# Layer 3 attention of a four-layer gated network: order of scores, last sums, projections and tokens within a step

## The chip, the cores and the metric

The kernel runs on one core of one Trainium2 chip. The metric is device time in microseconds (us) for one execution of the whole program; lower is better. Engines are named as in the profile: PE is TensorE's matmul, PEld its weight load, DVE is VectorE, ACT is ScalarE, POOL is GpSimd, SP is SyncE, which issues most of the DMAs.

## The reference

The input is 128 sequences of 64 tokens of width 128, with a context of the same size. Four layers follow one another, each a gated cross attention on the context and then a gated feed-forward part. The attention of layer 3 has 16 heads of width 8 and, in place of softmax, a "stablemax":

```python
def stablemax(x):
    s = jnp.where(x >= 0, x + 1.0, 1.0 / (1.0 - x))
    return s / jnp.sum(s, axis=-1, keepdims=True)
q = query @ Wq.T + bq          # query: the layer norm of x
k = key_value @ Wk.T + bk      # key_value: the context
v = key_value @ Wv.T + bv
scores = jnp.einsum('bhqd,bhkd->bhqk', q, k) / np.sqrt(HD).astype(np.float32)
attn = stablemax(scores)
context = jnp.einsum('bhqk,bhkd->bhqd', attn, v)
return context @ Wo.T + bo
```

The result, times tanh of a gate, is added to x. The feed-forward part of layer 3 sends each token to one of eight experts, up to a capacity; its routing (a layer norm, logits, the best expert, a place in that expert's list) is computed per tile while the attention runs, and its expert stage starts when all tokens are scattered to their slots. The input x of layer 3's attention is itself the sum of x and two rows per token that layer 2's experts wrote.

## The kernel before, in words

x stays on the chip as 64 tiles of 128 tokens (two sequences each). Layer 3's attention (`head_steps`, the branch `layer == 3`) runs a loop over n. A step n, also called a half, covers two tiles, that is four sequences with all heads; there are 32 such steps. Two steps share a group g of four tiles, for which the projections are made: `head_tokens` (normalized tokens xn by POOL, L719; adding the output bias to x by POOL, L726; and the DMA that loads the context ctxT of the group after, L177), `head_transpose` (pxn on PE, L734, xnT on ACT, L736), `head_queries` (pq on PE, L761, two copies qm on ACT, L764), `head_keys` (pk on PE, L773, two operations kx on DVE, L776) and `head_new_values` (pv on PE, L785, four copies vb on ACT, L792). `piece(n, late)` puts one of these into each half of a step. Before the change an even step holds tokens and the transpose in its first half and the new values in its second; an odd step holds the queries and then the keys. They are for the group after the one whose scores are in work.

The work of a step itself is: 16 score matmuls into four PSUM tiles sb (L875); four operations low on DVE, the negative part of the scores (L882); for each of the four quarters j a Ln and an Exp on ACT (L889, L891), which make 1 / (1 - x), and a sum on DVE (L894), which adds the positive part and leaves the weights aT. For the step before (n - 1) the same step computes the values pav (L908) from aT, raw on ACT (L913), the transposes po (L924), the reciprocal r and o on DVE (L930, L941), the transposes pot (L948), oT on ACT (L950), the output py (L968), and on DVE the addition to x (L970) and the statistics st (L200) of two tiles.

Two more streams are laid into the steps by lists of due times: `outputs`, the sums of x with layer 2's expert rows on POOL (L1884), their statistics gst on DVE (L1899, L1903), a group variance gn on DVE, its root on ACT and the norms gn_r (L260); and `first`, the routing of groups of 16, 8 or 4 tiles: variance and norms on DVE, tokens fxn on POOL (L1086), transposes prt (L1525) and logits plg (L1534) on PE, rT on ACT (L1527), the choice and the places on DVE with pup on PE (L1135). `scatter` puts the DMAs that carry routed tokens to their slots on POOL (L1646).

PE, ACT and DVE execute layer 3's attention in the order in which the program writes it (`manual_schedule`); the order on POOL and SP is chosen by the scheduler at build time. PSUM holds five buffers for score tiles and a ring of three ("av") for all the others in the stage.

Of the kernel before, what the change touches and what calls it, by code (L numbers as in the profile page):

```python
# [41 lines left out]
class Net:  # L42
# [536 lines left out]
    def head_steps(self, layer, w, NH):  # L579


        proj, mT, aT, raw, o = {}, {}, {}, {}, {}
        self.ctxT = {}
        self.context(0)

        def piece(n, late):

            g, step = (n // 2 + 1, n % 2) if layer == 3 else ((n + 3) // 2, (n + 1) % 2)
            if 4 * g >= self.NT:
                return  # L590
            if g not in proj:
                proj[g] = {}
                self.head_tokens(g, layer, w, proj[g])
            step = 2 * step + late
            if layer == 3:
                step = (0, 3, 1, 2)[step]
            if step == 0:
                self.head_transpose(g, proj[g])
            elif step == 1:
                self.head_queries(g, w, proj[g])  # L600
            elif step == 2:
                self.head_keys(g, w, proj[g])
                if layer == 2:
                    self.head_mask(g, proj[g])
            else:
                self.head_new_values(g, w, proj[g])

        proj[0] = {}
        outputs = {}
        if layer != 2:  # L610
            outputs = self.outputs_plan(layer)
            for step in sorted(outputs):
                if step[0] < (-2 if layer == 3 else 0):
                    for do in outputs.pop(step):
                        do()
        self.head_tokens(0, layer, w, proj[0])
        self.head_transpose(0, proj[0])
        self.head_keys(0, w, proj[0])
        if layer == 2:
            self.head_mask(0, proj[0])  # L620
        self.head_queries(0, w, proj[0])
        self.head_new_values(0, w, proj[0])
        if layer == 3:


            first = self.first_plan(3)
            for n in range(-2, NH + 8):
                for do in outputs.pop((n, 0), ()):
                    do()
                new, old = 0 <= n < NH, 0 <= n - 1 < NH  # L630
                if new:
                    st = self.head_stable(n, proj[n // 2])
                    self.head_stable_exp(st, 0)
                if old:
                    raw = self.head_values(n - 1, aT.pop(n - 1))
                if new:
                    self.head_stable_exp(st, 1)
                    self.head_stable_sum(st, 0)
                    piece(n, False)
                if old:  # L640
                    o = self.head_back(layer, raw)
                for do in first.pop(2 * n, ()):
                    do()
                self.scatter(2 if n < NH else 16)
                if new:
                    self.head_stable_sum(st, 1)
                    self.head_stable_exp(st, 2)
                if old:
                    oT = self.head_turn(o)
                if new:  # L650
                    self.head_stable_sum(st, 2)
                    self.head_stable_exp(st, 3)
                    piece(n, True)
                if old:
                    self.head_output(n - 1, layer, w, oT)
                    if n % 2 == 0:
                        self.first_fill(2 * n - 4)
                for do in first.pop(2 * n + 1, ()):
                    do()
                self.scatter(2)  # L660
                if new:
                    self.head_stable_sum(st, 3)
                    aT[n] = st["aT"]
                for do in outputs.pop((n, 1), ()):
                    do()
            return
        piece(-1, False)
        piece(-1, True)
        mT[0] = self.head_maxima_T(0, self.head_maxima(0, proj[0]))
        choice = self.choice_plan() if layer == 2 else {}  # L670
        scatter = self.scatter if layer == 2 else lambda n: None
        for n in range(NH + 8):
            for do in outputs.pop((n, 0), ()):
                do()
            if n + 1 < NH:
                mx = self.head_maxima(n + 1, proj[(n + 1) // 2])
            if 0 <= n - 1 < NH:
                raw[n - 1] = self.head_values(n - 1, aT.pop(n - 1))
            if n < NH:
                piece(n, False)  # L680
            if 0 <= n - 2 < NH:
                self.head_output(n - 2, layer, w, o.pop(n - 2))
            for do in choice.pop(2 * n, ()):
                do()
            scatter(3 if n < NH else 16)
            if n < NH:
                aT[n] = self.head_softmax(n, proj[n // 2], mT.pop(n))
            if 0 <= n - 1 < NH:
                o[n - 1] = self.head_back(layer, raw.pop(n - 1))
            if n < NH:  # L690
                piece(n, True)
            for do in choice.pop(2 * n + 1, ()):
                do()
            scatter(2)
            if n + 1 < NH:
                mT[n + 1] = self.head_maxima_T(n + 1, mx)
            if 0 <= n - 1 < NH and layer != 2:
                o[n - 1] = self.head_turn(o[n - 1])
            for do in outputs.pop((n, 1), ()):
                do()  # L700
# [162 lines left out]
            self.tc.add_manual_dep(exp.ins, self.table, ORDER, reason="the table is loaded")  # L863
        return aT

    def head_stable(self, n, pr):


        nc, work = self.nc, self.work
        b0 = 4 * (n % 2)  # L870
        sc = [self.ps_sc.tile([P, 4, 2, S], F32, tag="sc", name="sb") for j in range(4)]
        for b in range(4):
            for j in range(4):
                rows = slice(32 * j, 32 * j + 32)
                nc.tensor.matmul(  # L875
                    sc[j][:, b], lhsT=pr["kx"][rows, b0 + b], rhs=pr["qm"][rows, b0 + b],
                    start=True, stop=True,
                )
        lows = []
        for j in range(4):  # L880
            low = work.tile([P, 4, 2, S], F32, tag="low", name="low", bufs=4)
            nc.vector.tensor_scalar(low, sc[j], 0.0, -1e19, ALU.min, ALU.max)  # L882
            lows.append(low)
        aT = work.tile([P, 4, 4, 2, S], F32, tag="aT", name="aT")
        return {"sc": sc, "low": lows, "aT": aT}
# [756 lines left out]
    def scatter(self, n):  # L1642

        nc, tc = self.nc, self.tc
        for rec, row in self.ready[:n]:
            put = nc.gpsimd.indirect_dma_start(  # L1646
                out=self.scatter_dst, out_offset=bass.IndirectOffsetOnAxis(ap=row, axis=0),
                in_=rec, in_offset=None,
            )

            tc.declare_no_dep(put.ins, group=self.scatter_group, reason="rows apart")
            tc.add_to_no_dep_group(self.scatter_group, put.ins)
            for clear in self.scatter_after:
                tc.add_manual_dep(put.ins, clear, WAIT, reason="slots are clear")
            if self.pool_last:
                tc.add_manual_dep(put.ins, self.pool_last, ORDER, reason="GpSimd in this order")
            self.puts.append(put.ins.name)
            self.bundle.append(put.ins.name)
        del self.ready[:n]
# [315 lines left out]
```

## Time and profile before

| | us |
|---|---|
| median of 10 runs | 2862.94 (2859.89 to 2864.77) |
| the profiled execution, its own time | 2868.76 |
| its span on the core | 2866.7 |
| PE busy in the span | 2286.6 (80%) |
| DVE busy | 1571.0 (55%) |
| ACT busy | 1348.5 (47%) |
| POOL busy | 1056.8 (37%) |
| first and last low of layer 3 (start) | 2309.7 and 2675.0 |

The mean granted TensorE clock of the execution is 0.885 of full speed. Durations below come from this one execution; its time lies 5.8 us above the median of the runs.

A line of the groups or of the timeline names the engine, the line of the program, the operation, and what is written and read, as out<-in. In the timeline the first number is the start in the span and the second the duration; a bracket gives the idle time of the engine before it and what ended it. The view of the waits names who waited, for whom, the total, the number of times and the longest.

### The profile page before, as it was taken

Reading aid. Unit: us, or ns where it says so; the run is one execution under the profiler, and the core shown is the slowest. Engines: PE = TensorE matmul, PEld = TensorE weight load, DVE = VectorE, ACT = ScalarE, POOL = GpSimd, SP = SyncE. Lnnn points to the kernel's source line nnn. Section 1 sums busy time; section 2 is a strip of 40 time slices with the busy share of each in tenths; the row PEclk is TensorE's granted clock in tenths of the full one; section 3 lists DMA queues with packets and bytes.
Section 4 is the critical chain, followed back from the end, with each engine's and each line's share of the span. In section 5 each row is a group of like instructions: output and inputs, shape, how many; then the busy total and the mean of one; then the engine's idle time right before and its main releaser. Section 6 shows DMA issues by size and latency. Waiting matters only on the chain.

```text
span 2866.7 us, 68765 instructions
## 1 busy us (share of the span) xinstructions
PE 2286.6 (80%) x28510; PEld 1637.4 (57%) x28510; DVE 1571.0 (55%) x4232; ACT 1348.5 (47%) x2626; POOL 1056.8 (37%) x1297
## 2 busy tenths in 40 slices
PE   4999999999959778983556888884798666777597
PEld 3666666666647557772334666663566445555465
DVE  4445555554542276658874455455455377867532
ACT  2444444444424245555773444442344357665342
POOL 1222233332344521105653134425455652344344
PEclk9999999999979889995778998896899878877599
DMA  9983000000011310000000011111222530101111
GB/s 256 262 226 69 12 21 23 13 24 13 20 51 60 116 39 17 21 10 8 1 1 19 23 36 49 42 33 56 66 75 68 141 94 27 50 27 39 46 53 45
DMA packets 216582, 161.30 MB, mean 56 GB/s; under 512 B 27333, under 2 KB 192080, under 8 KB 216273
## 3 DMA queue, kind: packets, MB, share of 16 engines
q1 hardware_dynamic: 194288, 121.55, 16.4%
q0 software_dynamic: 16640, 32.22, 3.4%
q8 instruction: 226, 3.70, 0.5%
q10 hardware_dynamic: 5344, 3.15, 0.4%
q14 instruction: 84, 0.68, 0.1%
HBM read 68.62 MB, written 86.31 MB: 54 GB/s over the span
## 4 chain that ended last, share of the span: by engine, by line
PE 51%; DVE 15%; POOL 10%; issue 8%; ACT 8%; DMA 6%; SPq 1%; POOLq 0%; DVEq 0%; ACTq 0%
PE pqk L398 8%; PE pv L421 8%; PE py L480 4%; POOL slots L1646 3%; PE sc L440 2%; PE pt L468 2%; PE sb L850 2%; PE ph L1199 2%; PE pav L908 2%; DMA xe<-slots 2%; DMA outs<-ye,to 2%; PE pye L1218 2%; PE sb L857 2%; PE po L924 1%; POOL h L1384 1%
## 5 line engine op out<-in xcount | busy, mean ns | idle before, releaser
L457 POOL TENSOR_TENSOR a<-a,sm 128x1024 f32<-128x1024 f32 x64 | 121.7, 1902 | 490.5 <-DVE sm L456 449.4
L421 PE MATMUL pv<-Wvo,ctxT 128*64 128x512 f32 x1024 | 247.8, 605 | 0.0
L862 ACT ACTIVATE aT<-sb 128x512 f32<-128x512 f32 x256 | 132.1, 602 | 190.6 <-PE sb L857 190.6
L823 DVE TENSOR_REDUCE mpad<-sa 128x8 f32<-128x512 f32 x256 | 158.9, 683 | 111.5 <-PE sa L818 111.5
L447 DVE TENSOR_REDUCE mx<-sc 128x8 f32<-128x512 f32 x128 | 82.4, 685 | 229.3 <-PE sc L440 229.3
L1812 POOL DMA_INDIRECT outs<-ye,to x136 | 133.7, 983 | 132.0 <-DVE ye L1808 101.3
L428 ACT COPY v<-pv 128x512 f32<-128x512 f32 x128 | 75.2, 587 | 179.8 <-PE pv L421 179.7
L1646 POOL DMA_INDIRECT slots<-x_sb,fc_r x128 | 125.1, 977 | 82.3 <-DVE fc_r L1146 31.2
L908 PE MATMUL pav<-aT,vb 128*32 128x64 f32 x6144 | 130.0, 240 | 31.2 <-DVE aT L894 19.1
L719 POOL TENSOR_SCALAR xn<-x_sb,gn_nm,gn_r 128x128 f32<-128x128 f32 x128 | 58.4, 470 | 247.7 <-PE pxn L734 173.4
L1646 POOL DMA_INDIRECT slots<-x_sb,pl_i x64 | 61.6, 963 | 216.8 <-DVE pl_i L1631 163.5
L480 PEld LDWEIGHTS py<-v,aT 128*64 128x64 f32 x2048 | 117.5, 138 | 36.6 <-issue 19.4
L908 PEld LDWEIGHTS pav<-aT,vb 128*32 128x32 f32 x6144 | 109.3, 122 | 50.4 <-DVE aT L894 22.0
L398 PE MATMUL pqk<-xnT,L_Wq 128*128 128x256 f32 x512 | 121.1, 390 | 15.3 <-ACT xnT L390 14.9
L398 PE MATMUL pqk<-ctxT,L_Wk 128*128 128x256 f32 x512 | 121.4, 391 | 13.7 <-issue 13.7
L1769 PE MATMUL ph<-L_gu,xT 128*128 x272 | 130.5, 604 | 0.1
L402 ACT ACTIVATE kT<-pqk 128x512 f32<-128x512 f32 x128 | 76.4, 597 | 110.7 <-PE pqk L398 110.7
L1218 PEld LDWEIGHTS pye<-L_w,hT 128*128 128x128 f32 x1024 | 119.1, 192 | 14.4 <-issue 11.5
L480 PE MATMUL py<-v,aT 128*64 128x128 f32 x2048 | 124.2, 275 | 0.2 <-ACT aT L471 0.2
L1218 PE MATMUL pye<-L_w,hT 128*128 128x128 f32 x1024 | 119.2, 275 | 0.0
L930 DVE RECIPROCAL r<-po 128x32 f32<-128x32 f32 x96 | 34.3, 357 | 154.5 <-PE po L924 154.5
L1199 PE MATMUL ph<-xeT,L_w 128*128 128x512 f32 x256 | 118.3, 606 | 0.0
(325 smaller groups left out, 5828.1 us busy)
## 6 DMA issues: line engine op xcount, KB each, us to landing
slots<-zero SPq DMA_DIRECT2D x80, 528.0 KB, 9.1
ctxT<-in_ctxT_dram SPq DMA_DIRECT2D x64, 256.0 KB, 2.6
y<-outs SPq DMA_DIRECT2D x24, 512.0 KB, 5.4
xe<-slots SPq DMA_DIRECT2D x136, 66.0 KB, 1.9
xe<-slots SPq DMA_DIRECT2D x32, 264.0 KB, 2.8
L_w<-in_L_ffn_W_dram SPq DMA_DIRECT2D x32, 256.0 KB, 6.0
outs<-fxn SPq DMA_DIRECT2D x16, 256.0 KB
out_dram<-x_sb SPq DMA_DIRECT2D x16, 256.0 KB, 2.7
```

Source lines behind the costliest of these rows:

```text
L398: nc.tensor.matmul(ps[:, cc, :], lhsT=wt[:, (c + cc) * P : (c + cc + 1) * P], rhs=rhs, start=True, stop=True,)
L421: nc.tensor.matmul(ps[h * S : (h + 1) * S], lhsT=tok, rhs=w["Wvo"][:, h, cs, :], start=True, stop=True,)
L457: op = nc.gpsimd.tensor_tensor(ah, ah, sm.unsqueeze(2).to_broadcast([P, 16, S]), ALU.mult)
L480: nc.tensor.matmul(py[rows, :], lhsT=aT[:, c, rows], rhs=v[:, b, c, :], start=(c == 0), stop=(c == 7))
L823: nc.vector.reduce_max(mpad[:, j, 0:8], sc[j].rearrange("p b c k -> p (b c) k"), axis=AX.X)
L862: exp = nc.scalar.activation(aT[:, j], sc[j], AF.Exp)
L908: nc.tensor.matmul(pav[32 * j : 32 * j + 32, b, t, :], lhsT=vb[:, 4 * (b0 + b) + j, t, :], rhs=aT[:, j, b, t, :], start=True, stop=True,)
L1199: nc.tensor.matmul(ph, lhsT=w["w1"][:, e, c * P : (c + 1) * P], rhs=x, start=True, stop=True)
L1218: nc.tensor.matmul(py[:, t, :], lhsT=h[:, c, t * P : (t + 1) * P], rhs=w["w2"][:, e, c, :], start=(c == 0), stop=(c == 3),)
L1646: put = nc.gpsimd.indirect_dma_start(out=self.scatter_dst, out_offset=bass.IndirectOffsetOnAxis(ap=row, axis=0), in_=rec, in_offset=None,)
L1769: nc.tensor.matmul(ph.rearrange("p t f -> p (t f)"), lhsT=xT[j // 4][:, j % 4, :], rhs=gu[:, bass.ds(ex[j], 1), :, :].rearrange("p o t f - ...
L1812: put = nc.gpsimd.indirect_dma_start(out=self.outs2, out_offset=bass.IndirectOffsetOnAxis(ap=to[q][:, j % 4 : j % 4 + 1], axis=0), in_=y[: ...
```

## The change

Within a step the following is placed differently.

- The scores of step n + 1 are written at the end of step n, in front of the late piece; `head_stable` takes them ready.
- The pieces are no longer permuted. An even step holds the transpose and then the queries; an odd step the keys and then the new values.
- The late piece stands at the end of the step, behind the output of n - 1, the second half of the routing and the scores.
- Sum 1 stands in front of the first half of the routing, sum 3 in front of the output's addition to x and the second half of the routing.
- The tokens of a group are made at the end of the odd step before, behind the outputs list.

```diff
             step = 2 * step + late
-            if layer == 3:
-                step = (0, 3, 1, 2)[step]
             if step == 0:
                 self.head_transpose(g, proj[g])
...
             first = self.first_plan(3)
+            scores = None
             for n in range(-2, NH + 8):
                 for do in outputs.pop((n, 0), ()):
                     do()
                 new, old = 0 <= n < NH, 0 <= n - 1 < NH
                 if new:
-                    st = self.head_stable(n, proj[n // 2])
+                    st = self.head_stable(scores)
                     self.head_stable_exp(st, 0)
                 if old:
                     raw = self.head_values(n - 1, aT.pop(n - 1))
...
                 if old:
                     o = self.head_back(layer, raw)
+                if new:
+                    self.head_stable_sum(st, 1)
                 for do in first.pop(2 * n, ()):
                     do()
                 self.scatter(2 if n < NH else 16)
                 if new:
-                    self.head_stable_sum(st, 1)
                     self.head_stable_exp(st, 2)
                 if old:
                     oT = self.head_turn(o)
                 if new:
                     self.head_stable_sum(st, 2)
                     self.head_stable_exp(st, 3)
-                    piece(n, True)
+                    self.head_stable_sum(st, 3)
+                    aT[n] = st["aT"]
                 if old:
                     self.head_output(n - 1, layer, w, oT)
...
                 for do in first.pop(2 * n + 1, ()):
                     do()
                 self.scatter(2)
+                if 0 <= n + 1 < NH:
+                    scores = self.head_scores(n + 1, proj[(n + 1) // 2])
                 if new:
-                    self.head_stable_sum(st, 3)
-                    aT[n] = st["aT"]
+                    piece(n, True)
                 for do in outputs.pop((n, 1), ()):
                     do()
+                g = (n + 1) // 2 + 1
+                if n % 2 and n < NH and 4 * g < self.NT:
+                    proj[g] = {}
+                    self.head_tokens(g, layer, w, proj[g])
             return
```

`head_scores` is the first half of the old `head_stable`, the 16 matmuls; `head_stable` keeps the four operations low.

More of the change, by code (lines that the diff above doesn't have):

```diff
@@ L864, in head_softmax, with head_scores @@
         return aT
-    def head_stable(self, n, pr):
-        nc, work = self.nc, self.work
+    def head_scores(self, n, pr):
         b0 = 4 * (n % 2)
@@ L874, in head_stable @@
                 rows = slice(32 * j, 32 * j + 32)
-                nc.tensor.matmul(
+                self.nc.tensor.matmul(
                     sc[j][:, b], lhsT=pr["kx"][rows, b0 + b], rhs=pr["qm"][rows, b0 + b],
@@ L878, in head_stable @@
                 )
+        return sc
+    def head_stable(self, sc):
+        nc, work = self.nc, self.work
         lows = []
```

## The prediction

> **What bounds the kernel now.** I read the page first: the chain that ended last runs through all engines, so no engine is full and the stage must be read by its waits.
>
> ```profile
> PE 51%; DVE 15%; POOL 10%; issue 8%; ACT 8%; DMA 6%; SPq 1%; POOLq 0%; DVEq 0%; ACTq 0%
> ```
>
> The steps of layer 3 lie between 2308 and 2684 us of the span. Of those 376 us a step has 376 / 32 = 11.75. The view of who waited for whom, for that stretch:
>
> ```profile
> ACT low L889 <- DVE low L882: 74.3, 32, 6.1
> ...
> DVE aT L894 <- ACT low L891: 29.4, 24, 2.1
> ...
> PE pxn L734 <- POOL xn L719: 13.3, 6, 3.8
> ...
> PE sb L875 <- DVE kx L776: 12.6, 12, 2.3
> ```
>
> The columns are the total, the times, the longest. ScalarE stands still once per step (74.3 / 32 = 2.3 us) until VectorE has made the first low of the next step; VectorE in turn waits for Exp in most steps. So a step is one loop: low, Ln/Exp of four quarters on ACT, the last sum and the tail on DVE, low again. The timeline of steps 6 (even, from 2374.33) and 7 (odd, from 2382.19), which hold no routing, shows its parts:
>
> ```profile
> 2374.33 2.48 DVE L882 TENSOR_SCALAR low<-sb 128x512 f32<-128x512 f32 x4 [0.25 <-PE sb L875]
> 2375.06 0.63 ACT L889 ACTIVATE low<-low 128x512 f32<-128x512 f32 x1 [3.60 <-DVE low L882]
> ...
> 2378.78 1.06 PE L785 MATMUL pv<-L_xattn_Wv,ctxT 128*128 128x128 f32 x8
> ...
> 2379.59 0.35 ACT L950 COPY oT<-pot 128x256 f32<-128x256 f32 x1
> ...
> 2380.00 0.71 PE L968 MATMUL py<-wog,oT 128*128 128x128 f32 x4 [0.16 <-ACT oT L950]
> 2380.51 0.63 ACT L891 ACTIVATE low<-low 128x512 f32<-128x512 f32 x1
> 2380.64 1.17 PE L875 MATMUL sb<-qm,kx 32*128 32x128 f32 x32
> ...
> 2381.04 1.49 ACT L792 COPY vb<-pv 64x256 f32<-64x256 f32 x4
> ...
> 2381.60 0.67 DVE L894 SCALAR_TENSOR_TENSOR aT<-sb,low 128x512 f32<-128x512 f32 x1
> ...
> 2382.19 2.47 DVE L882 TENSOR_SCALAR low<-sb 128x512 f32<-128x512 f32 x4
> ...
> 2385.91 1.43 ACT L764 ACTIVATE qm<-pq,bqm,m2s 128x512 f32<-128x512 f32 x2
> ...
> 2389.16 1.52 DVE L776 TENSOR_SCALAR kx<-pk,L_xattn_bk,mc 128x512 f32<-128x512 f32 x2
> ```
>
> The even step takes 7.86 us, the odd one 10.62: in the odd one qm stands in the middle of ACT's run, kx in DVE's tail. The vb copies of the even step are free: pv was ready early, and they end while ACT waits for low anyway.
>
> **What moves on PE.** By the order of the instructions the scores of n+1 stay where they were: behind py (and plg, prt) of step n. What moves is the late piece (pv or pq), from in front of py to behind the scores. "A step ahead" thus advances the scores only where kx or a slow pv held them.
>
> **Odd steps, gain.** All times from the step's first low. qm's two copies leave ACT's run (1.33 to the next Ln), but kx now stands on DVE ahead of the reciprocal: sum 0 starts at 2.41, +0.66 kx, +1.43 reciprocal, +0.39 o, +0.43 and 0.45 through pot, so oT starts at 5.86 where it started at 6.24. Exp 3 then ends at 5.86 + 0.25 + 0.67 + 0.63 = 7.41; sum 3, add and two stats take 1.54: the tail (gst, norms) begins at 8.95 where it began at 9.84. Gain 0.89.
>
> **Even steps, loss.** Before, add and stats filled the time until Exp 3; now sum 3 is in front and DVE stands still for it. Exp 3 ends at 6.81; with 1.57 behind it low comes at 8.38 instead of 7.86. Loss 0.52. A pair gains 0.37 by these two.
>
> **The late copies, a new wait.** qm (even) and vb (odd) now wait on ACT for a matmul behind the scores, and the next step's Ln is queued behind them; so is all of Exp, and by it the sums. Even: oT ends at 5.61, py and scores at 7.48, pq 1.12, qm 1.36: the next Ln may start at 9.96, while low allows it at 8.38 + 0.73 = 9.11. Wait 0.85. Odd: oT ends at 6.22, scores at 8.09, pv and vb 2.55: 10.64 against 9.68. Wait 0.96. A DVE tail of that length hides it; without the tail all of it is paid: an even step passes it on whole, an odd one by 0.6 (low to low 8.95 with Ln at 0.73, 9.45 with Ln at 1.58). Those are full-clock durations. At half clock py takes 1.06 and the scores 2.09 (+1.27), and pq about 2.0 (+0.9): the wait is then 2.1 to 3.1.
>
> **The clock.** Windows of one 3.41 us period each:
>
> ```profile
> 2365.45:2368.86 3.41, 1.51 (x8) 0.89 (x8) 2.68 (x6) 3.35 (x7) 0.00 (x0) 1.00 0.00 0
> 2368.86:2372.28 3.42, 1.98 (x9) 0.98 (x8) 2.24 (x4) 2.54 (x5) 0.00 (x0) 0.50 0.26 77
> 2372.28:2375.69 3.41, 3.41 (x88) 3.19 (x92) 3.06 (x10) 0.63 (x1) 1.43 (x4) 0.50 0.02 5
> 2375.69:2379.10 3.41, 2.13 (x33) 1.59 (x26) 3.10 (x6) 3.32 (x7) 3.33 (x7) 1.00 0.00 0
> ```
>
> Behind the length stand the busy times (and counts) of PE, PEld, DVE, ACT and POOL, then the granted clock, the DMA share and GB/s. A period with PE busy for 1.51 us of 3.41 (44%) was followed by half clock, a full one by full clock. After the change py, scores, pq or pv, pav and pxn or pk stand in one block (0.7 + 1.2 + 1.1 + 1.1 + 0.7), and some 3.6 us with only po and pot (0.66 + 0.41, 30%) follow. A period that falls into these is thinner than the 44%, so I take the block's first matmuls, py and scores, at half clock in some 65% of the steps; now the score rows of the timeline show 2.0 to 2.1 in 12 of 32 steps, 1.4 to 1.8 in 5 more.
>
> [...]
>
> **Sum, steps 1 to 9.** Tails behind the stats are 0, 0.86, 1.83, 0.57 in turn. Four steps 4 to 7 at full clock: +0.6, -1.1, +0.9, -0.4 = 0. With every score run at half clock +4. I take +2.5 per four steps: +5.
>
> **Sum, steps 10 to 28 (routing).** Steps 10, 18, 22 and 26 are held by pxn waiting for POOL (up to 3.8 us), after which pv at half clock (1.9 us) holds py. Now pv is out of the way, and by POOL's order xn stands four fxn (1.74) earlier in steps 10 and 22 and two x_sb adds (1.28 each) earlier in 18: -2.7, -3.9, -1.1, -1.6, together -9. Of the nine odd steps six gain 0.8 to 1.4 each, since a tail hides the copies; 11, 19 and 27, which carry plg and prt in front of the scores, lose 0.3 each: together -6. The six other even steps have tails of 1.3 to 5 us; there sum 3 in front costs 0.5, and the inherited wait 0.7 to 1.7: +9. Half clock where the copies bind, nine steps by 0.9: +8. Sum +2; bounds -9 and +15.
>
> **Sum, steps 29 to 31.** No late piece remains; sum 3 of step 31 no longer stands behind 3.3 us of placing and norms, though po's successors then wait for fxn: -2.5, between -3.4 and 0.
>
> **At nothing.** Sum 1 in front of the routing: Exp 1 has ended at 3.8 and the reciprocal and o hold DVE until 4.15, so it waits for nothing; the routing behind it comes 0.65 later, and its readers wait for POOL or the next step. The ctxT load goes out a step earlier and waits on SP for pv of its own step; the output fills behind it have the rest of the stage as cover, the load itself four steps; without cover it would be its 2.6 us landing, once per pair. Tokens on POOL start when gn_r is ready, as now (67.4 us of wait there). Three PSUM buffers go round: po takes the one that qm or vb frees, 2 us earlier; behind plg and prt pv takes the one that the x add frees, now 0.65 later: 0 to 0.65 in three steps.
>
> Total +5 + 2 - 2.5 = +4.5 us. The profiled execution took 2868.76 (span 2866.7), 5.8 above the median of 2862.94; the sum is a difference and goes onto the median: 2867.5. Full clock throughout gives 0 - 9 - 2.5 = about -12, half clock +9 + 15 - 2 = +22. A measurement of this kernel tells 0.2% (5.7 us) from no change.
>
> **Rivals.** *Slower: Ln behind the late copies at half clock in nearly every step.* Midway between this sum and the half-clock bound: +14, 2877. It decides once the score runs take 2.09 us in more than three steps of four. For it: the thin stretch is as long as a period. Against it: a cold block lasts 8 us and so always contains a full period. *Faster: clock stays up and the copies land under DVE's tails.* -12, 2851. For it: over 20 of 32 steps have tails longer than 0.8. Against it: the wait needs only plg or prt (0.96, 0.63) in front of the scores to outlast them. *The scores' move does nothing:* on PE they hardly move, so without the late copies' cost only -0.37 per pair and the ends stay, -6 - 2.5; that lies between the other two and is counted with the faster one.
>
> **Numbers.** Forecast (terms cancel within -6 to +8): 0.42; slower rival 0.33; faster 0.25. Of the forecast 0.07 lies below -0.2%, 0.11 above +0.2%. Faster 0.32, same 0.24, slower 0.44. The range 2850 to 2884 leaves a tenth out on each side; the forecast's own range is 2857 to 2871.
>
> **What would show it.** Even steps without routing at 9 to 10 us and odd ones at 9.5 to 10.4, so that the two are nearly alike; ACT's wait for low (74.3) mostly replaced by one for pq and pv; PE's wait for kx gone; sum 3 right behind the last Exp; steps 10 and 18 some 3 us shorter. It is wrong if Ln starts 0.73 behind low in most steps, or if score runs are at full clock throughout.

## The result and the profile after

The changed kernel takes 2886.74 us (median of 8 runs, 2885.85 to 2893.05); the kernel before took 2862.88 beside it (28 runs, 2858.04 to 2867.46). The ratio is 1.0089, with a 95% interval of 1.0080 to 1.0097: the medians are 23.9 us apart, and the changed kernel lies 2.7 us above the upper end of the predicted range. The profiled execution of the changed kernel took 2887.61 us (span 2885.6). Its lines carry other numbers: low is now L892, Ln and Exp L899 and L901, sums L904, scores L879, qm L771 after pq L768, vb L799 after pv L792, py L978.

PE's share of the chain that ended last is 55%, where it was 51%:

```profile
PE 55%; DVE 14%; POOL 9%; ACT 8%; DMA 6%; issue 6%; SPq 1%; POOLq 0%; DVEq 0%; ACTq 0%
```

The waits of 2300 to 2710 us of the span (total, times, longest):

```profile
DVE aT L904 <- ACT low L901: 79.1, 63, 2.5
...
ACT vb L799 <- PE pv L792: 59.5, 15, 5.5
...
ACT qm L771 <- PE pq L768: 55.7, 15, 5.7
PE po L934 <- ACT raw L923: 40.4, 28, 3.5
...
ACT low L899 <- DVE low L892: 3.8, 4, 1.8
```

ScalarE's wait for low (74.3 before) has shrunk to 3.8. In its place stand 115 us for pv and pq, one wait in each of 30 steps, and behind it everything else is late: the sums on DVE wait 79.1 us for Exp (29.4 before), the po transposes 40.4 us for raw (23.3 before). The timeline of step 6 (even, low from 2378.79) and the start of step 7 shows why:

```profile
2378.79 2.48 DVE L892 TENSOR_SCALAR low<-sb 128x512 f32<-128x512 f32 x4
...
2380.17 1.50 ACT L799 COPY vb<-pv 64x256 f32<-64x256 f32 x4 [3.34 <-PE pv L792]
...
2381.70 0.63 ACT L899 ACTIVATE low<-low 128x512 f32<-128x512 f32 x1
...
2383.65 0.66 PE L934 MATMUL po<-ident,raw 128*128 128x128 f32 x4 [1.90 <-ACT raw L923]
...
2385.31 0.41 PE L958 MATMUL pot<-ident,o 128*128 128x128 f32 x2 [1.00 <-DVE o L951]
...
2386.36 0.35 ACT L960 COPY oT<-pot 128x256 f32<-128x256 f32 x1
...
2386.77 1.22 PE L978 MATMUL py<-wog,oT 128*128 128x128 f32 x4 [1.05 <-ACT oT L960]
...
2387.92 2.09 PE L879 MATMUL sb<-qm,kx 32*128 32x128 f32 x32
...
2389.94 1.13 PE L768 MATMUL pq<-xnT,L_xattn_Wq 128*128 128x512 f32 x2
2390.03 2.48 DVE L892 TENSOR_SCALAR low<-sb 128x512 f32<-128x512 f32 x4 [0.55 <-PE sb L879]
...
2391.11 1.45 ACT L771 ACTIVATE qm<-pq,bqm,m2s 128x512 f32<-128x512 f32 x2 [3.20 <-PE pq L768]
...
2392.45 0.62 ACT L899 ACTIVATE low<-low 128x512 f32<-128x512 f32 x1
```

A step is now a ring between ACT and PE: the first Ln (2381.70) to the end of oT (5.01 us), py and scores (3.30), pq and then qm, and the next Ln (2392.45), 10.75 us in all. ACT runs without a pause from the Ln to oT, so DVE is no longer in the ring: Ln starts 2.91 and 2.42 us after low has started, where it followed 0.73 behind in the kernel before. And py and scores run in a half-clock window. The windows between the clock's own boundaries (busy time and count of PE, PEld, DVE, ACT, POOL; granted clock; DMA share; GB/s):

```profile
2369.44:2372.86 3.42, 2.30 (x54) 1.26 (x45) 2.06 (x4) 3.33 (x9) 0.00 (x0) 1.00 0.02 7
2372.86:2376.27 3.41, 1.10 (x8) 0.72 (x6) 2.98 (x6) 2.72 (x6) 0.00 (x0) 1.00 0.00 0
2376.27:2379.68 3.41, 3.41 (x40) 3.12 (x39) 2.71 (x9) 0.56 (x1) 0.63 (x2) 0.50 0.00 0
2379.68:2383.10 3.42, 2.08 (x72) 1.62 (x71) 1.66 (x4) 2.81 (x7) 3.42 (x7) 1.00 0.27 81
2383.10:2386.51 3.41, 1.07 (x6) 0.62 (x6) 2.01 (x5) 3.35 (x7) 1.90 (x3) 1.00 0.00 0
2386.51:2389.92 3.41, 3.15 (x36) 2.73 (x36) 2.18 (x5) 1.37 (x3) 0.00 (x0) 0.50 0.00 0
```

It repeats in most steps: a window with po and pot (1.1 us of 3.4 busy) is granted full clock, and the next one is at half; that one holds the scores with py or pv, PE is busy for 3.15 and 3.41 us of it, and the clock is full again for the windows behind it (PE busy for 2.08 and 1.07 us from 2379.68 on). Between the first low of step 0 and that of step 31, 58 of 113 windows are at half clock, where 48 of 106 were before: a little more, but what changed most is what lies in them. Of the score runs of steps 2 to 31, 27 take 2.0 us or more ("cold" below, which means at half clock), where 12 did.

The lengths of the steps, from first low to first low, show where the time went (us, the predicted differences beside the measured ones; "filled" is the fourth experiment below). They add up to more than the 18.9 us by which the two profiled spans differ, since layer 3 starts 3.2 us earlier in the changed kernel's execution and what follows step 31's first low is 2.1 us shorter; the profiled execution of the kernel before was itself a long one.

| steps | before | predicted | changed - before | changed, filled - before |
|---|---|---|---|---|
| 0 | 14.90 | | -1.0 | -1.1 |
| 1 to 9 | 91.7 | +5 | +13.8 | +5.6 |
| 10 to 28 | 231.7 | +2 (-9 at full clock) | +12.0 | -8.4 |
| 29 and 30 | 25.2 | -2.5 (29 to 31) | -0.5 | -3.1 |
| sum | | +4.5 | +24.2 | -7.0 |

### The profile page after: what moved, and what is told of

Read it like the earlier page. It is cut to its first block, busy times and chain, and to the rows that moved or that the text cites. A ratio compares the mean times of both kernels' runs of the same rounds, so it can differ in the third digit from the quotient of the medians.

```text
span 2885.6 us, 68754 instructions
## 1 busy us (share of the span) xinstructions
PE 2306.0 (80%) x28510; PEld 1649.5 (57%) x28510; DVE 1568.3 (54%) x4232; ACT 1350.3 (47%) x2626; POOL 1056.9 (37%) x1297
## 3 DMA queue, kind: packets, MB, share of 16 engines
q10 hardware_dynamic: 5344, 3.15, 0.4%
## 4 chain that ended last, share of the span: by engine, by line
PE 55%; DVE 14%; POOL 9%; ACT 8%; DMA 6%; issue 6%; SPq 1%; POOLq 0%; DVEq 0%; ACTq 0%
PE pqk L398 8%; PE pv L421 8%; PE py L480 4%; PE sb L857 3%; PE sc L440 2%; PE pt L468 2%; PE ph L1209 2%; PE sb L864 2%; DMA xe<-slots 2%; PE pye L1228 2%; PE pav L918 2%; DMA outs<-ye,to 2%; POOL slots L1656 2%; DVE mpad L830 2%; PE sb L879 2%
## 5 line engine op out<-in xcount | busy, mean ns | idle before, releaser
L904 DVE SCALAR_TENSOR_TENSOR aT<-sb,low 128x512 f32<-128x512 f32 x128 | 86.7, 686 | 79.2 <-ACT low L901 79.1
L1228 PEld LDWEIGHTS pye<-L_w,hT 128*128 128x128 f32 x1024 | 119.1, 192 | 14.3 <-issue 11.5
L918 PE MATMUL pav<-aT,vb 128*32 128x64 f32 x6144 | 117.1, 232 | 11.7 <-ACT vb L799 6.6
L918 PEld LDWEIGHTS pav<-aT,vb 128*32 128x32 f32 x6144 | 100.0, 118 | 42.5 <-issue 14.1
```

What stands on the lines that cost most here:

```text
L918: nc.tensor.matmul(pav[32 * j : 32 * j + 32, b, t, :], lhsT=vb[:, 4 * (b0 + b) + j, t, :], rhs=aT[:, j, b, t, :], start=True, stop=True,)
L1228: nc.tensor.matmul(py[:, t, :], lhsT=h[:, c, t * P : (t + 1) * P], rhs=w["w2"][:, e, c, :], start=(c == 0), stop=(c == 3),)
```

## Experiments

Theories: A, ScalarE's order (Ln behind copies that wait for a matmul behind the scores); B, the sums in front of the residual, or the new order of the pieces; C, the clock of the PE block. Each kernel was timed in turns with the kernel before. The ratios compare best between runs; us are the ratio's distance from 1 times 2863. GpSimd's order is chosen at build time and could change with any edit; in the traces it is the same, instruction by instruction, in the changed kernel and in kernels 1, 3, 4, 6, 8 and 9, so it does not part these. Kernel 5 has the order of the kernel before; kernels 2, 7 and 11 share a third order, kernels 10 and 12 a fourth.

| | median us | ratio (95%) | us against before | score runs of 2.0 or more, steps 2 to 31 |
|---|---|---|---|---|
| changed kernel | 2886.7 | 1.0089 (1.0080 to 1.0097) | +25.5 | 27 |
| 1 late piece in front of py | 2849.9 | 0.9951 (0.9938 to 0.9963) | -14.0 | 6 |
| 2 sums back | 2892.0 | 1.0089 (1.0076 to 1.0102) | +25.5 | 27 |
| 3 copies later on ACT | 2881.5 | 1.0053 (1.0040 to 1.0065) | +15.2 | 23 |
| 4 changed, filled | 2855.1 | 0.9965 (0.9953 to 0.9977) | -10.0 | 1 |
| 5 before, filled | 2863.5 | 1.0002 (0.9993 to 1.0011) | +0.6 | 0 |
| 6 kernel 1, filled | 2854.2 | 0.9966 (0.9954 to 0.9978) | -9.7 | 1 |
| 7 kernel 1, sums back | 2858.9 | 0.9990 (0.9980 to 1.0001) | -2.9 | 6 |
| 8 changed, a third filled | 2877.8 | 1.0054 (1.0041 to 1.0068) | +15.5 | 5 |
| 9 late piece between py and scores | 2868.5 | 1.0016 (1.0007 to 1.0026) | +4.6 | 12 |
| 10 before, sums in front | 2870.0 | 1.0021 (1.0011 to 1.0031) | +6.0 | 11 |
| 11 kernel 1, sum 3 back | 2859.1 | 0.9979 (0.9970 to 0.9989) | -6.0 | 7 |
| 12 kernel 1, tokens back | 2851.5 | 0.9949 (0.9936 to 0.9963) | -14.6 | 4 |

**1. The late piece alone put back**

```diff
                     self.head_stable_sum(st, 3)
                     aT[n] = st["aT"]
+                    piece(n, True)
...
-                if new:
-                    piece(n, True)
```

> The changed kernel with one part undone: the late piece (pq and qm in even steps, pv and vb in odd ones) is issued in front of the output projection again, right behind the last Exp and sum 3; scores, sums, the new order of the pieces and the tokens stay as changed. Theory A (the lost time is ScalarE's queue: the next step's Ln stands behind copies whose matmul waits behind the scores): Ln starts 0.73 us behind low again in most steps, ScalarE's waits for pq and pv (55.7 + 59.5 us in the changed kernel) go to under 15, and the time falls from 2886.7 to 2858-2868. Theory B (the sums in front of the residual, and the new order of the pieces, are what costs): the time stays within 6 us of 2886.7. Theory C (TensorE's clock: the block of py, scores, pq or pv runs at half clock): pv and pq go back into the thin stretch, so the score runs should be at 2.09 us in fewer steps than the 28 of 31 now; if they stay at 2.09 and the time falls all the same, the clock was not the main cost.

Measured 2849.9, a ratio of 0.9951: below A's range, so not only the loss goes, but what is left of the change gains 14 us. The waits of this kernel, 2300 to 2710 us:

```profile
ACT low L898 <- DVE low L891: 44.3, 31, 3.6
DVE aT L903 <- ACT low L900: 37.0, 38, 2.2
...
ACT qm L770 <- PE pq L767: 2.8, 1, 2.8
```

The 115 us for pq and pv are 3.0, Ln starts 0.70 to 0.73 us behind low in every step, and the sums' wait for Exp is down from 79.1 to 37.0. Step 6 takes 8.42, step 7 10.33. The score runs of 2.0 or more are down to 6: order and clock moved together, so this alone does not part A from C. The new order of the pieces, which this kernel keeps, is not what costs.

**2. Sums 1 and 3 put back in the changed kernel**

> The changed kernel with sum 1 put back behind the routing and sum 3 back behind the residual add, stats and routing (as before the change); all else as changed. Theory A (late copies): 2884-2888, since ScalarE still waits for pq and pv and the sums have slack; by the prediction's term (0.52 us lost per even step without tail, sum 1 at nothing) at most 8 us less, 2878-2887. Theory B (sums in front of the residual): 2863-2872, with VectorE's wait of aT for Exp falling from 79.1 us to about 30.

Its ratio is that of the changed kernel to the fourth digit. B's first half is out: behind the late copies the place of the sums, with the order on POOL that goes with it, makes no difference in sum.

**3. PE's order kept, the copies taken out of Ln's way.** `late` holds the qm or vb copies of the step before.

```diff
                     self.head_stable_exp(st, 1)
+                    if late:
+                        late()
+                        late = None
                     self.head_stable_sum(st, 0)
```

> The changed kernel, TensorE's order untouched (the late matmul behind the scores), but ScalarE's qm and vb copies are issued behind Ln/Exp 0, the raw copy and Ln/Exp 1 of the next step, so that no Ln stands behind them. Theory A (queue order on ScalarE): Ln starts 0.73 us behind low in nearly every step and the 115 us of waits for pq and pv vanish; the copies now cost 1.4 us of ScalarE's run in the middle of every step, so 2868-2880, some 6 to 18 us better than the changed kernel. Theory C (half clock itself): low comes as late as before since the scores still take 2.09 us, and the time stays within 6 us of 2886.7, or is slower by the copies (up to 2900).

By the ratios 10 us better than the changed kernel; the median stands just above A's range and just inside C's. The waits for pq and pv are all but gone and the old one is back, but the copies now stand in front of oT, for which PE waits (22.8 us in the changed kernel):

```profile
ACT low L914 <- DVE low L907: 71.5, 32, 4.9
...
PE py L993 <- ACT oT L975: 43.5, 31, 2.7
```

ScalarE's order counts, but freeing it here brings back less than half of the time, with 23 score runs still cold.

**4. The clock held up, the order untouched.** The same call stands in front of pot with 4 and of py with 8.

```diff
         po = self.ps_av.tile([P, 4, P], F32, tag="av", name="po")
+        if layer == 3:
+            self.keep_busy(po, 6)
...
+    def keep_busy(self, ps, count):
+        for i in range(count):
+            self.nc.tensor.transpose(ps[:, i % 2, :], self.ident, self.ident)
```

> The changed kernel with extra TensorE transposes of the identity in front of po (6), pot (4) and py (8), into the same PSUM tiles, which the real matmuls then overwrite: 18 of some 0.165 us at full clock, 3 us per step in the thin stretch. They do nothing for the output. Theory C (the clock of the block): the windows of the steps are granted full clock, score runs go from 2.09 to 1.17 us, py from 1.2 to 0.7, and the time falls to 2848-2862, the prediction's full-clock sum (-12 against the kernel before). Theory A alone (the order on ScalarE's queue costs also at full clock): score runs go to 1.17 but the time falls only to 2868-2880. If the extra matmuls do not lift the clock, or delay po, pot and py, 2886-2910.

2855.1: PE does 2.5 us more per step, and the kernel is 35.5 us faster than the changed one (0.9965 against 1.0089). The windows of the same stretch:

```profile
2370.86:2374.27 3.41, 1.75 (x16) 1.52 (x15) 3.07 (x6) 2.45 (x6) 0.00 (x0) 1.00 0.02 5
2374.27:2377.68 3.41, 3.41 (x107) 3.01 (x106) 2.68 (x9) 1.44 (x4) 0.60 (x2) 1.00 0.00 0
2377.68:2381.10 3.42, 2.78 (x27) 1.97 (x18) 2.42 (x5) 3.29 (x7) 3.42 (x7) 1.00 0.30 81
2381.10:2384.51 3.41, 2.69 (x31) 2.10 (x33) 1.96 (x4) 3.35 (x7) 1.97 (x3) 1.00 0.00 0
```

No window there is at half clock, the mean granted clock of the execution is 0.905 where the changed kernel's is 0.881, and one score run of steps 2 to 31 takes over 2.0 us where 27 did. The waits for pq and pv fall to 71.1 us but remain:

```profile
ACT vb L799 <- PE pv L792: 38.7, 15, 4.1
...
ACT qm L771 <- PE pq L768: 32.4, 15, 3.8
```

Steps 5 and 6 take 9.28 and 9.23 us; the even and odd step before, 7.86 and 10.62, average 9.24. At full clock the ring of ACT and PE costs nearly what the old loop cost: steps 4 to 7 take 39.4 us where they took 38.8.

**5. The kernel before, filled in the same way**

> The kernel before, with the same 18 extra transposes of the identity per step (6 in front of po, 4 of pot, 8 of py; 2.5 us at full clock), which the real matmuls overwrite. Theory C (clock): its score runs at 2.09 us, 12 of 32, go to 1.17, and the time falls by some 12 x 0.9 to 12 x 1.4 = 11 to 17 us at most, to 2848-2860; then the change is even or a little better once the clock is taken out (the changed kernel with them took 2855.1). Rival: the extra matmuls work by something other than the clock (they were worth 31.6 us in the changed kernel), and then the kernel before gains about as much, 2832-2842; or they stand in the way of po, pot and py where its late piece already fills the stretch: 2866-2880.

No difference (1.0002), though none of the 12 cold score runs is left; the expectation was wrong. Steps 11 and 19, for one, are 1.0 and 0.7 us shorter, but steps 2 and 6 take 8.51 instead of 7.87 and 7.86: the extra transposes stand in the way by 0.65 us there. So the extra work has a price, and the 35.5 us of kernel 4 are what is left after it. That some of the cold score runs were free here can be read from single steps: in steps 3, 13 and 17 the scores fall from 2.09 to 1.17 us, and the steps keep their lengths within 0.03 us, as do steps 7 and 15, where they take 1.17 and 1.37 without the transposes.

**6. Kernel 1, filled (6, 4 and 2 transposes)**

> The late piece in front of the output projection (the version that took 2849.9), with extra transposes: 6 in front of po, 4 of pot, 2 of py. Seven of its score runs still took 2 us or more. Theory C: those go to 1.17 and the time falls by 5 to 10 us, to 2838-2846, the best so far. If the late copies' place matters at full clock too (the filled changed kernel is 2855.1), this one lies 8 to 17 us below that one. Rival: clock was only a passenger and the stretch is full already: 2848-2858.

Not faster than kernel 1, so the expected 2838 to 2846 was wrong, and equal to kernel 4 (0.9966 and 0.9965). Whether kernel 1's six cold score runs had slack or the price of the transposes ate their gain, no run shows. With the clock up, the late piece in front of py or behind the scores makes no difference within some 5 us, the price of the extra transposes, which is not the same in the two, included; in steps 4 to 7 it makes 1.6 us (37.8 against 39.4). So most of what A costs, it costs by way of C.

**7. Kernel 1 with sums 1 and 3 back; 11. with sum 3 alone back**

> The changed kernel with the late piece in front of the output projection and sums 1 and 3 where they were before the change: what is left of the change is the new order of the pieces, tokens at the end of odd steps and the scores emitted a step ahead. Theory: with ScalarE free of the late copies the sums in front of the residual either cost (the prediction's 0.52 per even step: 2842-2848) or, as e2 with its +5.3 says, gain (2853-2860). If the whole gain of the 2849.9 version is the sums': 2860-2868.

> The version that took 2849.9 (late piece in front of the output projection) with sum 3 alone put back behind residual, stats and routing; sum 1 stays in front of the routing. With both back it took 2858.9. By the two traces the 9 us are POOL's order in steps 10 and 22 (8.4 against 11.7 us, and 10.8 against 12.7), which goes with sum 3: 2855-2862, and even steps without routing 0.4 us shorter than 8.42. If sum 1 is what pays: 2846-2851.

0.9990 and 0.9979 against 0.9951: about 8 us belong to sum 3, with the order on POOL that goes with it, and sum 1's share (0.0011) is inside the intervals. Step 6 takes 8.00 in both against 8.42 in kernel 1, so in plain even steps sum 3 in front costs 0.42; it gains elsewhere, above all in step 10 (8.41 us in kernel 1, 12.00 with sum 3 back). POOL, first with sum 3 in front (kernel 1), then with sum 3 back (kernel 11):

```profile
2415.68 1.73 POOL L1095 TENSOR_SCALAR fxn<-x_sb 128x128 f32<-128x128 f32 x4 [34.87 <-DVE gn_t L257]
2417.40 1.73 POOL L725 TENSOR_SCALAR xn<-x_sb,gn_nm,gn_r 128x128 f32<-128x128 f32 x4
```

```profile
2418.08 3.51 POOL L1096 TENSOR_SCALAR fxn<-x_sb 128x128 f32<-128x128 f32 x8 [33.15 <-DVE x_sb L1508]
2421.57 2.16 POOL L726 TENSOR_SCALAR xn<-x_sb,gn_nm,gn_r 128x128 f32<-128x128 f32 x5
```

POOL's order is not written by hand: moving one sum on DVE puts xn in front of four fxn or behind them. With it in front, pxn starts 1.83 us after step 10's first low, with it behind 2.96; of the remaining 2.5 us of the step much is clock again (pq 1.02 against 1.91, py 0.61 against 1.06, prt likewise), so how the 8 us divide between POOL's order and the clock's phase stays open.

**8. A third of the extra work (8 transposes in front of py)**

> The changed kernel with only the 8 extra transposes in front of py (1.04 us at full clock, 2.1 at half), where the 18 gave -31.6 us. Theory C: less work in the thin stretch lifts the clock in fewer steps; with some half of the score runs at 1.17 the time is 2865-2878, and steps with a full-clock score run are 1 to 2.5 us shorter than the same steps of the changed kernel. If 8 are enough to keep the clock, 2852-2860. If they do not lift it, they run at half and hold py: 2887-2905.

10 us better than the changed kernel, inside the expected range, with 5 score runs of 2.0 or more and 8 between 1.35 and 1.9. The eight transposes take 1.7 us per step and not 1.04, since 197 of the 256 run at half clock (0.42 us against 0.27 each), and they hold py, which stays at half clock in three steps of four. So steps 3 and 7, whose scores are now faster (1.44 and 1.17 us), are no shorter (11.67 and 11.68 against 11.63 and 11.25), and that part of the expectation was wrong: the number of cold score runs alone does not give the time.

**9. The late piece between py and scores**

> The changed kernel with two neighbours on TensorE exchanged: the late piece stands behind the output projection and the routing's matmuls, but in front of the next scores; all else as changed, POOL's order too. Theory A (it is the scores in front of the copies' matmul that costs): Ln starts 0.73 us behind low, the waits for pq and pv fall below 40 us, 2850-2862. Theory C (the place in the thin stretch counts, since py, pq or pv and the scores then still form one cold block): score runs stay at 2.09 us in over 20 of 32 steps, what Ln no longer waits for, low waits for instead (the scores now stand behind 2 us of pq or pv), and the time stays at 2872-2890.

+4.6 us, between both ranges: some 21 us less than the changed kernel, some 19 more than kernel 1. Ln starts 0.72 behind low, as A says, though the waits for pq and pv are still 57.7 us where A had under 40. Cold score runs are 12, where C had over 20; but as C says, low now waits for the scores behind pq or pv:

```profile
DVE low L892 <- PE sb L879: 38.7, 25, 4.7
...
ACT vb L799 <- PE pv L792: 31.4, 15, 3.5
```

Of low's wait 11.5 us were there in the changed kernel. By the times of the three kernels, about half of the loss is the place behind the scores, half the place behind py, out of the thin stretch.

**10. The sums alone, in the kernel before**

> The kernel before with one part of the change alone: sum 1 in front of the routing, sum 3 right behind the last Exp, in front of the residual add. By the undoing runs (the sums were worth 5.3 and 9.0 us) the time falls by 4 to 10 us, to 2853-2859, if POOL's order changes with it in steps 10 and 22 (xn in front of four fxn). By the prediction's term (even steps lose 0.5 us, nothing gained) 2864-2872. If the sums pay only together with the new order of the pieces: 2860-2866.

Slower by 6 us. The first expectation was wrong; the time lies in the range that goes by the prediction's term, but not for that term's reason. POOL's order changes and steps 10 and 22 are 1.0 and 2.1 us shorter, but there kx stands at the end of the odd step, now behind sum 3, and the scores wait for it (26.7 us against 12.6); step 5 takes 12.10 instead of 10.65. In these runs the sums pay only together with the keys in the first half of the odd step.

**12. Kernel 1 with the tokens back at the start of even steps**

> The version that took 2849.9 (late piece in front of the output projection, sums in front) with the tokens put back to the start of even steps, as before the change. By GpSimd's order the move of the tokens sets four more of the output adds (x_sb from y, which wait for a transfer) ahead of the xn of step 2, and in all runs with the moved tokens step 2 takes 14 us where the kernel before takes 7.9; the first three steps together take 38 to 39 us against 33.7 to 35.6. Theory (the tokens cost there, contrary to the prediction's nothing): step 2 comes down to 8 to 9 us, the first three steps to 34 to 36, and the time to 2844-2848. If the early tokens pay it back in later steps: 2849-2856.

Step 2 falls from 14.23 to 8.43 us as expected, and the time stays (0.9949, 0.9951). The step's 5.8 us are given back in steps 10, 11, 16 and 18 (+2.4, +1.5, +2.9, +3.0): in step 10 the same matmuls now fall into half clock (pq 1.92 us against 1.02), in step 18 POOL has adds in front of xn, which is ready 2.5 us later. Kernels 1 and 12 have the lowest ratios of all versions, both below the kernel before and the changed one.

## Why the prediction was wrong

**The step that failed is the clock's price.** The text put py and scores at half clock in "some 65% of the steps" and took +2.5 of +4 us per four steps, and +8 in steps 10 to 28: 13 us in all. The trace has 27 of 30 steps there, and the lengths of the steps of the changed kernel and the filled one differ by 31.2 us. Steps 4 to 7 took 38.8 us before, 45.3 after and 39.4 with the clock held: +6.5 with half clock against a bound of +4, +0.6 without. The bound of +4 is 1.0 us a step, less than the 1.27 us by which the text itself has py and scores longer at half clock; it let a DVE tail hide the wait and an odd step pass on 0.6 of it. Measured, half clock costs about 1.5 us a step there: the ring of ACT and PE passes it on whole, and it is longer still where pq is cold too (10.75 us in step 6, 12.05 in step 4, whose pq takes 2.08). With the clock held the sum comes near: a total of -10.0 us against "about -12". From there to the changed kernel it is 35.5 us; the two bounds, -12 and +22, were 34 apart. The sum went between the bounds where the measurement, +25.5, lies a little beyond the upper one.

**The full-clock sum: steps 4 to 7 hold one by one, steps 10 to 28 only in sum.** The text had +0.6, -1.1, +0.9 and -0.4 for steps 4 to 7; kernel 4 measures +1.1, -1.4, +1.4 and -0.5, the price of its transposes included. For steps 10 to 28 it measures -8.4, where the text's lower bound is -9 and its terms without half clock give -6. That is in part luck: the four steps held by POOL gain 5.0 us and not 9 (4.5 in the changed kernel), the nine odd steps gain 10.5 and not 6, and the six other even ones lose 7.1 where the text had 9.

**The slower rival was the right case.** "It decides once the score runs take 2.09 us in more than three steps of four": they do. It was priced midway, +14, where its own bound of +22 was nearly it. The text held against it that "a cold block lasts 8 us and so always contains a full period". The windows above show why a full period does not help: the windows at 1.00 (2379.68 to 2386.51) follow the block's cold part and run on into po and pot, where PE is busy for 1.07 us of 3.41, and the next block's py and scores are at 0.50 again.

**The late copies: right in mechanism and near in size.** 2.1 to 3.1 us past the usual 0.73 were priced for half clock; in steps 6 and 7 it is 2.2 and 1.7, and the median of steps 2 to 28 is 2.2. More lateness sits in low itself, which in step 7 starts only when the scores end.

**Odd steps, gain 0.89: right in sign.** Kernel 7 against the kernel before is 0.70 us shorter in the mean of the odd steps 1 to 29, but in the plain steps 5 and 7, for which the term was worked out, by 0.01 and 0.04 only. In the changed kernel any gain is hidden: step 7 takes 11.25.

**Even steps, loss 0.52: right in place.** 0.42 between kernels 1 and 11. But sum 3's move as a whole gains 8 us where the copies are out of the way, part of it by POOL's order, which goes with it. The text had that gain (-2.7 and -1.1 in steps 10 and 22) without saying which edit brings it; in the changed kernel step 10 keeps 0.15 of it, step 22 1.5.

**At nothing: the tokens are nothing only in sum.** Step 2 is 6.4 us longer after the change, contrary to "Tokens on POOL start when gn_r is ready, as now". gn_r ends at 2329.99, but two output adds, which wait for a transfer, now stand in front of xn:

```profile
2332.66 1.27 POOL L1894 TENSOR_TENSOR x_sb<-x_sb,y 128x512 f32<-128x512 f32 x1 [4.58 <-DMA y<-outs]
2334.59 1.27 POOL L1894 TENSOR_TENSOR x_sb<-x_sb,y 128x512 f32<-128x512 f32 x1 [0.66 <-DMA y<-outs]
2335.85 2.15 POOL L726 TENSOR_SCALAR xn<-x_sb,gn_nm,gn_r 128x128 f32<-128x128 f32 x5
```

This is 6.4 of the 13.8 us in steps 1 to 9, and it was in reach, since the text goes by POOL's built order in other steps. With the late piece in front of py later steps pay it back (kernel 12); whether they do in the changed kernel itself, no run shows. Sum 1 at nothing is right within the intervals.

**The row at 44%: right.** The trace agrees with the row by which the sum went: in the changed kernel's steps the granted clock went from 1.00 to 0.50 29 times, each time after a window in which PE was busy for 19 to 67%. Another 26 full-clock windows, with PE busy for 51 to 100%, were followed by full clock, so between 51 and 67% the busy share alone does not tell. The longest idle time of PE is 1.90 us in step 6 and 3.54 us at most (from 2319.31, step 0 into step 1). It is the edit that puts the matmuls together that leaves the rest of the step too thin: 1.10 and 1.07 us of 3.41 busy in the rows above, each followed by a window at 0.50.

## What to carry to other kernels

Moving matmuls out of a thin stretch into a full one cost twice here: the block got longer, and the stretch left behind (PE busy for 1.1 us of 3.4) was followed by half clock for it; so ask of each PE move which window it empties. Ask also what stands behind the block: cold scores with slack were free (steps 3, 13 and 17 of the kernel before), while cold matmuls in front of a copy with Ln queued behind it were worth 35 us. Where a sum lies between a full-clock and a half-clock bound, ask first whether the pattern repeats with the step, and be slow to weigh the two by a share: this loop went to one side (27 of 30 cold), though others stayed mixed (12 of 30 in the kernel before and in kernel 9).

## What the runs showed of the hardware

Extra transposes made the changed kernel faster: 2.5 us more PE work per step took 1.2% off it (kernel 4), and nothing off the kernel before (kernel 5, 1.0002). In the steps of the changed kernel the granted clock went from 0.50 to 1.00 28 times, each time after a window in which PE was busy for 92% or more; the other 30 of its 58 half-clock windows were followed by another one at half clock, five of these with PE busy throughout.
